# First attention of a two-layer transformer kernel: other work set behind each score round instead of behind each pair of rounds, and the value matmuls set in two halves

## The chip, the core and the metric

The kernel runs on one core of a Trainium2 chip. The metric is the device time of one execution in microseconds (us). Three runs of the kernel before gave a median of 1532.57 us (1531.0 to 1534.91). The engines are named as the profile names them: PE (matmul), PEld (PE's weight load), DVE (vector), ACT (scalar, activations), POOL (GpSimd) and SP (it issues most of the DMAs).

## The reference

The input is x with 64 batch items of 128 tokens and 128 features, a side input `fside` of the same shape and a context `ctx_1024` of 64 x 120 x 128. Four blocks follow each other, each with a layer norm ahead and a residual sum behind. All is float32.

```
def _L0_xattn_ref(x1, x2, memory_k, memory_v, Wq, bq, Wk, bk, Wv, bv, Wp, bp):
    ...
    q = (x1 @ Wq + bq).reshape(Bn, Nq, H, D).transpose(0, 2, 1, 3)
    k = x2 @ Wk + bk
    v = x2 @ Wv + bv
    k = jnp.concatenate([k, memory_k], axis=1)
    v = jnp.concatenate([v, memory_v], axis=1)
    ...
    attn = jnp.einsum('bhqd,bhkd->bhqk', q, k) * scale
    attn = jax.nn.softmax(attn, axis=-1)
    out = jnp.einsum('bhqk,bhkd->bhqd', attn, v)
    ...
    return out @ Wp + bp
...
    x = x + _L0_xattn_ref(_layernorm(x, axis=-1), fside_BxSxS_0, ctx_1024, ctx_1024, ...)
    x = x + _L0_ffn_ref(_layernorm(x, axis=-1), L0_ffn_wqkv, L0_ffn_w1, L0_ffn_w2)
    x = x + _L1_xattn_ref(_layernorm(x, axis=-1), ctx_1024, ctx_1024, ...)
    x = x + _L1_ffn_ref(_layernorm(x, axis=-1), L1_ffn_Wg, L1_ffn_bg, L1_ffn_W1, L1_ffn_W2)
```

Both attentions have 16 heads of 8 features. The first one attends over 248 keys: 128 projected from `fside` and 120 taken from the context as they are. The second attends over 120 keys projected from the context. Both feed-forward blocks send each token to 2 of 8 experts. The change touches the first attention only.

## The kernel before

The kernel runs four stages after each other: loads, the first attention with the first router beside it, the first layer's experts ("tile stage"), and the second attention with the second layer's experts beside it. The order of PE, ACT, DVE and POOL is the order in which the program is written; SP's order is chosen by the framework's scheduler, except at the beginning and at the end of the first attention.

**The pipeline.** `attention` runs a loop over `it` from 0 to 68 (`B + 5` steps for 64 batch items). In each step several batch items are worked on at different depths: item `it` gets its row maxima, item `it-1` its shift, item `it-2` its scores and exponentials, item `it-3` its values and the first two output steps, item `it-4` its third and item `it-5` its last two. Batch items are grouped by four (`GB`), and the projections of the next group are spread over the four steps of a group.

**A round** (`round_`, calling `max_bank` L386 and `score_bank` L418) fills four PSUM banks by eight matmuls that use the PE array in four strips of 32 rows, so that four of them run side by side:

- two "left" banks: query x key for 248 keys (L394), of which DVE takes the negated maximum (`tensor_reduce`, L414) into `nm`,
- two "right" banks: key x query for one chunk of keys, 128 or 120 of them (L430), of which ACT takes the exponential into `p` (L438).

All first matmuls of the four banks are issued ahead of the second ones. A step has four rounds, 0 to 3, so 16 banks. PSUM has eight; every other PE result of the loop takes a bank of the same pool (`mtile`), too, and a bank becomes free when DVE or ACT has read it. Rounds 0 and 1 read the first key chunk, rounds 2 and 3 the second.

**The other work of a step**, with the lines that the prediction uses:

- `shift` (L459 on PE, L462 on DVE): transposes the maxima of item `it-1` and adds them to its queries by two `scalar_tensor_tensor`.
- `values` (L475): exponentials x values, in the array cut into four strips of 32 columns. `values(b, 0)` takes a bank and fills its first half, `values(b, 1)` its second half, 32 matmuls each. `out1` (L484) is ACT's copy of that bank.
- `out2` (L491 on PE, then L495 and L497 on DVE), `out3` (L504 on PE, L506 on ACT), `out4` (L511 on PE), `out5` (L516 on DVE, then the norm statistics L109).
- `aside.ahead` (one more L109 on DVE) and `aside.call`, twice a step: the next pieces of the router. Of PE they hold L176 (with ACT's copy L177) and L681 in one step of four, and L831 in one of eight; the rest is small DVE and POOL work, and POOL's scatters.
- `prep(it, 0)` and `prep(it, 1)`: the next group's projections. By `j = it % 4`: query projection (L292, with ACT's L301 twice in each of the two calls, and its bank held from the first call to the end of the second) at j=0, nothing at j=1, values (L214, DVE's L221) and keys (L202, ACT's L207) at j=2, turned inputs (L176, ACT's L177) at j=3.
- `context`: at j=2, the DMAs of the next group's context keys (L261) and values (L266). `aside.end` issues stores of zeros (L1278) from SP.

A step of the first attention runs: rounds 0 and 1; `out4`, `shift`, `out5`, `ahead`, a router call; both halves of the values and `out1`; `context`, `prep(it, 0)`, a router call; rounds 2 and 3; `out3`, `out2`, `prep(it, 1)`, `aside.end`.

Of the kernel before, what the change touches and what calls it, by code (L numbers as in the profile page):

```python
# [44 lines left out]
def transformer_kernel(ctx, tc, a, out):  # L45
# [186 lines left out]
    def attention(layer, w, norm, first, aside):  # L232
# [5 lines left out]
        with ExitStack() as es:  # L238
# [14 lines left out]
            def loads(g):  # L253
                n = KF if first else KC
                t = work.tile([D, GB, n], F32, name="kvT", tag="kvT")
                nc.sync.dma_start(t, a["fsideT" if first else "ctxT"][:, g * GB : (g + 1) * GB, :])
                src[g] = t
# [13 lines left out]
            def context(g):  # L271
                if first:
                    context_k(g)
                    context_v(g)
# [167 lines left out]
            def round_(ba, bc, rnd):  # L442


                one, two = ((0, 2), (1, 3)) if rnd % 2 == 0 else ((1, 3), (0, 2))
                left = [max_bank(ba, ra, rnd // 2) for ra in one] if ba is not None else []
                right = [score_bank(bc, ra, rnd // 2) for ra in two] if bc is not None else []
                banks = [x for pair in zip(left, right) for x in pair] if left and right else left + right
                for u in range(2):
                    for parts, _ in banks:  # L450
                        parts[u]()
                for _, after_ in banks:
                    after_()
# [12 lines left out]
            def values(b, v):  # L466
                g, j = divmod(b, GB)
                if v == 0:
                    pavs[b] = mtile()
                pav = pavs[b]  # L470
                p = ps_[b]
                for i in range(2):
                    for c, (_, n) in enumerate(chunks):
                        for ra in range(4):
                            nc.tensor.matmul(  # L475
                                pav[32 * ra : 32 * ra + 32, v * S : (v + 1) * S],
                                lhsT=vs[g % 2][c][:, j, 4 * v + ra, i, :],
                                rhs=p[:n, c, ra, (2 * v + i) * S : (2 * v + i + 1) * S],
                                start=(i == 0 and c == 0), stop=(i == 1 and c == nc_ - 1),
                            )  # L480
# [38 lines left out]
            def norm_of(g):  # L519
                if g < NG:  # L520
                    normed[g] = norm.normed(g)
                    biased(g)
# [30 lines left out]
            for it in range(B + 5):  # L553
                def on(back, *steps):
                    b = it - back
                    if 0 <= b < B:
                        for f in steps:
                            f(b)

                def rounds(*which):  # L560
                    ba = it if it < B else None
                    bc = it - 2 if 0 <= it - 2 < B else None
                    for r in which:
                        if ba is not None or bc is not None:
                            round_(ba, bc, r)

                if first and it % GB == 2:
                    norm_of(it // GB + 2)
                if 2 <= it <= B + 1 and it - 2 not in ps_:
                    ps_[it - 2] = work.tile([128, nc_, 4, 512], F32, name="p", tag="p")  # L570
                if it % GB == 0 and 0 < it // GB + 1 < NG:
                    if it:
                        loads(it // GB + 1)
                vals = (lambda b: values(b, 0), lambda b: values(b, 1), out1)
                if first:
                    rounds(0, 1)


                    on(5, out4)
                    on(1, shift)  # L580
                    on(5, out5)
                    aside.ahead(it)
                    aside.call(it, mtile)
                    on(3, *vals)
                    if it % GB == 2 and it // GB + 1 < NG:
                        context(it // GB + 1)
                    prep(it, 0)
                    aside.call(it, mtile)
                    rounds(2, 3)
                    on(4, out3)  # L590
                    on(3, out2)
                    prep(it, 1)
                    aside.end(it, work, mtile)
                else:
                    on(3, *vals)
                    rounds(0, 1)


                    aside.piece(mtile)
                    prep(it, 0)  # L600
                    on(4, out3)
                    on(3, out2)
                    on(5, out4)
                    aside.call(it, mtile)
                    prep(it, 1)
                    on(1, shift)
                    on(5, out5)
                    aside.ahead(it)
                    if it > GB and it % GB == 1:
                        norm_of(it // GB + 1)  # L610
                    aside.fetch_for(it)
                    aside.call(it, mtile)
                ps_.pop(it - 3, None)
                yield
# [676 lines left out]
    wr0 = const.tile([D, 3 * E], F32, name="c_wqkvT", tag="c_wqkvT")  # L1291
    aside0 = Aside0()
    steps = attention(0, l0, norms[0], True, aside0)
    next(steps)
    l0.update(attention_weights("a0_", ("wq", "bq")))
# [170 lines left out]
    with ExitStack() as es:  # L1466
        aside1 = Aside1(es.enter_context(tc.tile_pool(name="yb", bufs=1)))
        with tc.manual_schedule(engines=ORDERED):
            for _ in attention(1, l1, norms[2], False, aside1):
                pass  # L1470
# [91 lines left out]
```

## Time and profile before

| what | value |
|---|---|
| median of three runs | 1532.57 us |
| the profiled execution's own time | 1582.29 us |
| its span, first to last instruction | 1580.5 us |
| mean granted PE clock | 0.973 |
| busy share of the span: PE, PEld | 91%, 71% |
| busy share: DVE, ACT, POOL | 70%, 54%, 41% |
| L414 reduces of both attentions | 768, 465.4 us busy |
| L438 exponentials of both attentions | 768, 403.5 us busy |
| L430, L394 score matmuls, busy | 444.5 us, 294.3 us |
| L475 value matmuls on PE (p,v and p,vc), busy | 179.6 us, 104.2 us |

The span is one profiled execution; the runs that give the median were not profiled and are shorter. A busy PE is not PE at its peak, since matmuls overlap each other. The first attention's loop takes the span from about 30 us to about 630 us. There its steps repeat with a period of eight (two groups), which makes it possible to read one period and to multiply.

### The profile page before, as it was taken

The numbers are of one execution on the slowest core, as the hardware profiler recorded it, in microseconds if no ns is written. First come the engines' busy times: TensorE is split into PE (matmuls) and PEld (weight loads), VectorE is DVE, ScalarE is ACT, GpSimd is POOL, SyncE is SP. The second block draws the span as 40 slices with busy tenths as digits, with TensorE's granted clock in tenths as the row PEclk, the third lists the DMA queues.
The fourth block names the chain that finished last, engine by engine and source line by source line (L and its number), as shares of the span: only waits on it lengthen the run. The fifth ranks groups of instructions, "written<-read, shape, count | busy, mean of one in ns | idle before, by whom it ended". The sixth has DMA issues, their size and how long they took to land.

```text
span 1580.5 us, 41996 instructions
## 1 busy us (share of the span) xinstructions
PE 1442.8 (91%) x16620; PEld 1118.6 (71%) x16620; DVE 1106.3 (70%) x3024; ACT 849.7 (54%) x1740; POOL 641.3 (41%) x1195
## 2 busy tenths in 40 slices
PE   7969999999999999787999999888989898988987
PEld 5757777777777677676888888566666676666765
DVE  6757888888888988354654444688776777777763
ACT  4646666666666666442333333566656565655653
POOL 4122345646465534464001122376555555444210
PEclk9989999999999999899999999899999999999999
DMA  7851222222222221365776676111000111100000
GB/s 192 222 138 46 55 61 68 67 61 64 57 64 58 56 70 37 93 187 173 213 201 189 194 202 180 46 35 30 28 28 28 37 31 31 31 28 15 15 8 28
DMA packets 143719, 133.03 MB, mean 84 GB/s; under 512 B 48546, under 2 KB 126114, under 8 KB 141602
## 3 DMA queue, kind: packets, MB, share of 16 engines
q1 hardware_dynamic: 135330, 113.02, 25.9%
q0 software_dynamic: 8192, 17.32, 3.5%
q8 instruction: 132, 2.16, 0.6%
q14 instruction: 65, 0.53, 0.1%
HBM read 97.32 MB, written 32.97 MB: 82 GB/s over the span
## 4 chain that ended last, share of the span: by engine, by line
PE 66%; DVE 15%; DMA 6%; SPq 5%; issue 3%; ACT 3%; POOL 3%; another core or an unknown queue 0%; POOLq 0%; ACTq 0%; DVEq 0%
PE bank L430 10%; PE bank L475 9%; PE bank L1115 8%; PE bank L394 8%; PE bank L1420 4%; PE bank L1441 4%; DVE nm L414 3%; PE bank L1128 3%; DMA q<-xs 3%; SPq L1278 2%; PE bank L407 2%; PE bank L292 2%; DVE q L462 2%; PE bank L511 2%; PE bank L681 2%
## 5 line engine op out<-in xcount | busy, mean ns | idle before, releaser
L414 DVE TENSOR_REDUCE nm<-bank 128x2 f32<-128x496 f32 (+1 forms) x768 | 465.4, 662 | 100.6 <-PE bank L430 68.6
L438 ACT ACTIVATE p<-bank 120x512 f32<-120x512 f32 (+1 forms) x768 | 403.5, 603 | 154.9 <-PE bank L430 138.5
L430 PE MATMUL bank<-q,k 32*120 32x256 f32 (+1 forms) x3072 | 444.5, 401 | 14.8 <-DVE nm L414 5.0
L430 PEld LDWEIGHTS bank<-q,k 32*120 32x120 f32 (+1 forms) x3072 | 298.3, 182 | 61.9 <-DVE nm L414 16.6
L394 PE MATMUL bank<-k,q 32*128 32x248 f32 x2048 | 294.3, 403 | 12.5 <-DMA k<-in_ctx_k 11.8
L394 PEld LDWEIGHTS bank<-k,q 32*128 32x128 f32 x2048 | 203.1, 190 | 59.7 <-issue 23.0
L475 PE MATMUL bank<-p,v 128*32 128x128 f32 (+1 forms) x4096 | 179.6, 279 | 1.8 <-DVE h L1435 0.6
L1120 DVE TENSOR_TENSOR p<-p,bank 128x256 f32<-128x256 f32 x213 | 87.9, 420 | 125.4 <-ACT p L1119 112.6
L407 PE MATMUL bank<-k,qf 32*128 32x480 f32 x512 | 150.8, 604 | 1.3 <-ACT qf L295 0.8
L807 POOL DMA_INDIRECT xs<-xn,at x128 | 129.2, 1009 | 28.6 <-issue 25.0
L1119 ACT ACTIVATE p<-bank 128x256 f32<-128x256 f32 x213 | 80.9, 384 | 100.9 <-PE bank L1115 91.9
L484 ACT COPY ov<-bank 128x256 f32<-128x256 f32 x128 | 48.0, 375 | 157.5 <-PE bank L475 146.0
L475 PEld LDWEIGHTS bank<-p,v 128*32 128x32 f32 (+1 forms) x4096 | 111.2, 110 | 26.1 <-issue 13.2
L1115 PE MATMUL bank<-q 128*128 128x256 f32 x516 | 122.3, 388 | 4.6 <-ACT q L1106 4.6
L1360 POOL DMA_INDIRECT yb<-ys,back x112 | 108.7, 970 | 27.7 <-issue 19.3
L462 DVE SCALAR_TENSOR_TENSOR q<-bank,c_smask,q 128x256 f32<-128x256 f32 x256 | 111.1, 475 | 10.3 <-PE bank L459 9.6
L167 POOL TENSOR_SCALAR xn<-x,mv,rstd 128x128 f32<-128x128 f32 x252 | 110.6, 452 | 7.3 <-issue 1.3
L1115 PEld LDWEIGHTS bank<-q 128*128 128x128 f32 x516 | 97.4, 196 | 17.3 <-ACT q L1106 5.0
L155 POOL TENSOR_SCALAR rstd<-mv 128x4 f32<-128x4 f32 x32 | 6.4, 199 | 246.7 <-DVE mv L113 150.0
L475 PE MATMUL bank<-p,vc 120*32 120x128 f32 x2048 | 104.2, 272 | 0.6 <-issue 0.5
L1157 POOL DMA_INDIRECT kvT<-ys,back x16 | 15.4, 962 | 197.5 <-DMA vc<-xs 118.1
L301 ACT ACTIVATE q<-bank,c_a_bq,c_hmask 128x512 f32<-128x512 f32 x124 | 90.1, 788 | 9.8 <-PE bank L292 9.8
(224 smaller groups left out, 2477.6 us busy)
## 6 DMA issues: line engine op xcount, KB each, us to landing
q<-in_w SPq DMA_DIRECT2D x43, 576.0 KB
vc<-in_w SPq DMA_DIRECT2D x28, 576.0 KB
vc<-in_ctx_v SPq DMA_DIRECT2D x16, 960.0 KB
ys<-zero SPq DMA_DIRECT2D x71, 128.0 KB
k<-in_ctx_k SPq DMA_DIRECT2D x32, 240.0 KB
q<-xs SPq DMA_DIRECT2D x43, 128.0 KB
ys<-q SPq DMA_DIRECT2D x43, 128.0 KB
x<-in_x SPq DMA_DIRECT2D x16, 256.0 KB
```

The source lines that it names most:

```text
L167: nc.gpsimd.tensor_scalar(xn[:, j, :D], xg[g][:, j, :], self.mv[:, b, 0:1], self.rstd[:, b : b + 1], ALU.add, ALU.mult,)
L301: nc.scalar.activation(q4s[g][:, :, s, :], pq.rearrange("p (b q) -> p b q", b=GB), AF.Identity, bias=w["bq"][:, s : s + 1], scale=hmask[:, ...
L394: nc.tensor.matmul(pa[:, u, :], lhsT=q4s[g][r, j, s, :], rhs=k2[g % 2][r, s // 2, j, :], start=True, stop=True,)
L407: lambda: nc.tensor.matmul(pa, lhsT=qfs[g][r, j, :], rhs=k4s[g][r, :, j, :], start=True, stop=True),
L414: nc.vector.tensor_reduce(nm[b % 2].rearrange("q i (a s) -> q a i s", s=16)[:, 2 * ra + v : 2 * ra + v + len(slots) // 2, :, 0], pa.rearra ...
L430: nc.tensor.matmul(pb[:n, v * 256 : (v + 1) * 256], lhsT=k2[g % 2][r, v, j, k0 : k0 + n], rhs=q4s[g][r, j, 2 * v : 2 * v + 2, :].rearrange ...
L438: nc.scalar.activation(ps_[b][:n, c, ra, :], pb[:n], AF.Exp, scale=SCALE)
L462: nc.vector.scalar_tensor_tensor(q, pm, smask[:, v : v + 1], q, ALU.mult, ALU.add)
L475: nc.tensor.matmul(pav[32 * ra : 32 * ra + 32, v * S : (v + 1) * S], lhsT=vs[g % 2][c][:, j, 4 * v + ra, i, :], rhs=p[:n, c, ra, (2 * v + ...
L807: s = nc.gpsimd.indirect_dma_start(xs, bass.IndirectOffsetOnAxis(at[:, j, k : k + 1], 0), xn, None)
L1115: nc.tensor.matmul(ph[:, u, :], lhsT=w[:, c, u * 128 : (u + 1) * 128], rhs=xT, start=True, stop=True)
L1360: nc.gpsimd.indirect_dma_start(y[:, k, b % 2, :], None, ys, bass.IndirectOffsetOnAxis(back[:, b, k : k + 1], 0),)
```

## The change

Only the order of calls within a step of the first attention changes. Each round of four banks now stands alone, with a part of the other work behind it. The two halves of the values are separated by round 2, the second router call moves ahead of round 2, and `context` and `prep(it, 0)` stay behind the values, now between rounds 2 and 3. Nothing is computed that was not computed before.

```diff
                 if first:
-                    rounds(0, 1)
-
-
+
+                    rounds(0)
                     on(5, out4)
                     on(1, shift)
                     on(5, out5)
                     aside.ahead(it)
                     aside.call(it, mtile)
-                    on(3, *vals)
+                    rounds(1)
+                    on(3, vals[0])
+                    aside.call(it, mtile)
+                    rounds(2)
+                    on(3, *vals[1:])
                     if it % GB == 2 and it // GB + 1 < NG:
                         context(it // GB + 1)
                     prep(it, 0)
-                    aside.call(it, mtile)
-                    rounds(2, 3)
+                    rounds(3)
                     on(4, out3)
                     on(3, out2)
                     prep(it, 1)
```

`vals` is the triple of the first half of the values, the second half, and `out1`.

## Prediction, made before the changed kernel was run

> **What bounds the kernel now.** I read the page first: PE is busy for 91% of the span, DVE for 70%. Then I read the windows of two whole groups (four steps each) in the even part of the first attention, from one first value matmul to the next but three:
>
> ```profile
> 211.50:248.69 37.19, 36.76 (x570) 27.89 (x569) 31.82 (x80) 24.53 (x50) 20.41 (x42) 1.00 0.24 61
> 248.69:287.80 39.11, 37.77 (x574) 28.55 (x573) 32.94 (x86) 24.19 (x50) 20.57 (x49) 1.00 0.23 60
> ```
>
> The columns are window and length, then busy us of PE, PEld, DVE, ACT and POOL, granted clock, DMA share and GB/s. PE looks full (36.8 of 37.2), DVE has 31.8, ACT 24.5. But PE's busy time hides waiting, since matmuls overlap. So next I looked at the timeline of PE for a block of two rounds that nothing holds up:
>
> ```profile
> 242.55 0.47 PE L394 MATMUL bank<-k,q 32*128 32x248 f32 x1
> ...
> 242.86 0.37 PE L394 MATMUL bank<-k,q 32*128 32x248 f32 x1
> ...
> 243.07 0.37 PE L394 MATMUL bank<-k,q 32*128 32x248 f32 x1
> ...
> 244.14 0.37 PE L394 MATMUL bank<-k,q 32*128 32x248 f32 x1
> ...
> 244.45 0.33 PE L504 MATMUL bank<-ident,o 128*128 128x128 f32 x1
> ```
>
> Four matmuls start together; the first four take 0.31 us to the next four, then each 0.21, and the last 0.30 to the next operation. From 242.55 to 244.45 is **1.90 us for two rounds**. Most blocks take longer. The chain of waits says why:
>
> ```profile
> 289.76 1.05 PE bank L292 x2
> 290.82 0.40 PE bank L394
> ...
> 291.90 0.67 DVE nm L414
> 292.57 0.04 issue
> 292.62 0.47 PE bank L430
> 293.11 0.63 PE bank L430 x4
> 293.73 0.26 PE bank L504
> ```
>
> The last bank of rounds 2 and 3 had to wait until DVE had reduced a bank of this same block. From 292.62 the block still needs 1.1 us, as long as a round alone: PE issues in order, so one late bank delays the whole round. The block took 2.91. Rounds 0 and 1 wait for something else, DVE's queue:
>
> ```profile
> 302.21 2.42 DVE L414 TENSOR_REDUCE nm<-bank 128x2 f32<-128x496 f32 x4 [0.77 <-PE bank L430]
> 304.54 0.25 DVE L495 RECIPROCAL rs<-bank 128x16 f32<-128x16 f32 x1
> 304.83 0.29 DVE L497 TENSOR_TENSOR o<-bank,rs 128x128 f32<-128x128 f32 x1
> ```
>
> `out2`'s bank was filled by 303.5 and is free only at 305.1, because four reduces of 0.605 stand ahead of its two DVE steps.
>
> From the same timeline, the 16 blocks of the two groups take (first start to the next operation's start) 2.92, 2.95, 1.91, 2.77, 2.09, 2.66, 1.90, 2.41 and 2.92, 2.96, 1.91, 2.77, 3.37, 2.67, 1.91, 2.61. Over 1.90 each, that is **4.4 us of waiting in the first group and 5.9 in the second**, on average 5.2 of 38.15.
>
> **The change, part by part.**
>
> *Splitting the rounds.* One round alone is 0.31 + 0.21 + 0.21 + 0.30 = 1.03 us; two are 2.06 instead of 1.90. There are two such splits in a step: +0.32. *Splitting the values*: 64 matmuls take 1.90 (298.24 to 300.14 in the chain), at 0.11 for four 1.76, so 0.14 are the way in and out, and two halves pay it twice, about +0.13. Together **+0.45 us in a step, 1.8 in a group**. All of it lies on PE, the engine that sets the pace. The switch from strips of rows to strips of columns is not in the trace; its nearest rows are row strips to whole array (0.30 instead of 0.21) and whole array to column strips (L459 to L475, 0.20 instead of 0.11), so 0.09 to 0.18 above the pace. I take the lower one, as what leaves is the same; the upper adds 0.2 in a step.
>
> Here a rule speaks against the change. The Trainium skill, "TensorEngine Tiling (Array Packing)", section "Tiling Modes", says that changing the tiling mode drains TensorE. A plain step has 5 changes of mode before and 8 after. Taken at its word, nothing of the new mode begins until the last matmul has ended (0.37 after its start instead of 0.21) and the first weights are loaded (0.18): 0.34 a change, 1.0 a step, 4.1 a group. The trace shows less of it: from the last row-strip matmul to L504 are 0.30, weights included. I go by the row.
>
> *The waits.* I laid four steps out by hand from these durations: reduce 0.605 and exponential 0.53 in a row, the first 0.10 and 0.15 after a round's end (301.07 to 302.21 and 302.25 for a round of 1.03); shift's two DVE steps 0.78, `out5` 0.28, two statistics 0.49, reciprocal and product 0.54; 0.4 of router work on DVE for each call (the windows' 64.8 us of DVE for eight steps, less 58 for the named groups, over 16 calls); `out4` and `shift` 0.64 on PE, `out3` and `out2` 0.54; ACT's query steps 0.79 each. Each new bank takes the one longest free.
>
> - Plain step: round 3 ends at 0, round 0 would start at 0.54 and finds two banks free; its last two take round 3's first exponential and first reduce, free at 0.75: wait 0.1 to 0.2. `out4` and `shift` follow, then round 1, which takes the banks of `out3`, `out2` and two of round 0's, free 0.75 after it, when PE is there after 0.64: wait 0.1. Round 2 comes 2 us later and takes round 0's others, `shift`'s and `out4`'s: DVE frees these about 1.9 us after round 0 (two reduces, two shift steps, `out5`), no wait. Round 3 has the second half of the values ahead of it; DVE is through round 1's reduces 0.8 us earlier: no wait, and `out1` comes in time.
> - j=0: the query projection's bank is held over round 3 and to the end of its four ACT steps, and ACT does two of these ahead of round 3's exponentials and two behind. Of the following step round 0 waits 0.8 for the second reduce of round 3, and round 1 waits 0.7 for its fourth bank, since round 0's exponentials start 1.1 late.
> - j=2 into j=3: ACT's two key steps (L207, 0.78 each) hold up round 0's exponentials; round 1 waits 0.6.
>
> Sum over a group: 0.13+0.13 (j=0), 0.83+0.7 (j=1), 0.23+0.13 (j=2), 0.57 (j=3) = **2.7 us**, where 4.4 and 5.9 stood. The first group comes out at 37.19 - 4.4 + 2.7 + 1.8 = 37.3, the second at 39.11 - 5.9 + 2.7 + 1.8 = 37.7: **0.65 us less a group on average**. The bounds: no waiting at all (5.2 - 1.8 = 3.4 less) and waiting undiminished (1.8 more).
>
> *Moved work.* The second router call goes ahead of round 2: its DVE work now stands ahead of round 2's reduces, which have about 0.8 us to spare; L681 then gives DVE and ACT a microsecond there. `context` now waits for round 2 as well, about 1 us later in its step; its keys are read in round 0 two steps (18 us) on, its values later still, so nothing waits. The weight of ACT's idle time ahead of `out1` (83 us waiting for L475 in all) goes, worth nothing, as ACT isn't late there. The shift of item `it-1` now has one round less ahead of it: it needs round 3's reduces, done at 1.3 to 1.5 after round 3, and comes at 1.9; half a microsecond is left.
>
> *Where it counts.* Up to 95.6 us the loop doesn't run free. SP's queue:
>
> ```profile
> 52.67 39.79 SPq L1278 DMA_DIRECT2D ys<-zero  x63
> 92.56 1.04 SPq L261 DMA_DIRECT2D k<-in_ctx_k  x2
> ```
>
> The keys for step 8 are issued behind 63 stores of zeros; PE stands from 83.9 to 95.6. A faster or slower step ahead of it changes only that wait. So steps 8 to 63 count, 14 groups: 14 x 0.65 = **9 us less**. The profiled execution goes from 1582.3 (span 1580.5, 1.8 around it) to 1573. The 50 us by which it exceeds the median I can't place; as the attention runs at clock 1.00 in the profile, I carry the 9 us over: 1532.6 - 9 = 1524.
>
> **The rivals.**
>
> - *The waits all but vanish* and PE's own work with the splits is the bound: 14 x 3.4 = 48 less, 1485. For it: DVE (32.4 a group) and ACT are below PE. Against: at j=0 and j=2 ACT's extra steps stand in its queue whatever the order.
> - *The drain costs what the rule says* (slower): three more changes of mode a step at 0.34. The layout removes 0.62 us of waiting a step (5.2 - 2.7 over four), so the change loses once its switches cost more than that; at 1.0 it is 0.4 x 56 = 22 more, 1555. For it: the direct switch between row and column strips, twice a step, is in no row. Against: all rows of other switches.
> - *SP's order changes*: the scheduler may put the keys of step 8 ahead of the zeros, 11.7 us less on top, 1512, or more zeros ahead of some other load. Little speaks for it, as the zeros have no one to wait for in either order.
>
> **How the numbers follow.** Forecast (1524, its own range 1511 to 1536, as each wait of the layout may be off by 0.1 to 0.2 us): 0.54. No waits: 0.09. Drain: 0.32. SP's order: 0.05. What a measurement here can tell from no change is about 0.3%, 4.6 us. Of the forecast's share 0.33 is faster by more than that, 0.16 within and 0.05 slower; with 0.09 and 0.04 faster by the others, that makes 0.46 faster, 0.17 within and 0.37 slower (the drain's 0.32 in it). The range runs from 1500, halfway to the case without waits, to 1558, a little past the drain's.
>
> **What would show it.** In the profile after, a round alone takes 1.03 where it doesn't wait; the switch from L430 to L475 shows 0.30 (right) or 0.5 and more (drain). Waits of a round for DVE's L497 go; the long ones left stand at j=0 to j=1 and end with L414 or L301. The two groups become nearly equal in length. It is wrong if DVE is late for round 3 in plain steps, or if `shift` waits for `nm`.

## The result, and the profile after

The changed kernel is slower: 1551.14 us median of 4 runs (1549.27 to 1554.21) against 1532.88 for the kernel before beside it, ratio **1.0121 [1.0099, 1.0143]**. The forecast was 1524.

Its profiled execution took 1549.27 us with a span of 1547.4. One fact has to stand ahead of every comparison. The same unchanged kernel takes 1533 to 1536 us on some chips and 1581 to 1590 on others. By its time, the profile of before that the prediction works with (1582) belongs to the second kind; the median to be forecast, and the profile after, belong to the first. Profiling is not what makes the difference: the profiled execution of after is the fastest of its four. I call the two kinds **short-time** and **long-time** chips and compare only within a kind. A later run gave a profile of before on a short-time chip (own time 1533.83, span 1532.1), and it is what I set beside the profile after. Each engine's busy time, first of after, then of before on the short-time chip:

```profile
PE 1450.3 (94%) x16620; PEld 1100.3 (71%) x16620; DVE 1100.5 (71%) x3024; ACT 853.3 (55%) x1740; POOL 639.9 (41%) x1195
```

```profile
PE 1425.8 (93%) x16620; PEld 1110.9 (73%) x16620; DVE 1102.1 (72%) x3024; ACT 847.5 (55%) x1740; POOL 640.5 (42%) x1195
```

PE is 24.5 us busier, and the others do about as much as before. The windows of two whole groups show the same, in the same order (window and length, then busy us of PE, PEld, DVE, ACT and POOL, granted clock, DMA share, GB/s):

```profile
257.10:295.95 38.85, 38.30 (x576) 27.36 (x572) 32.77 (x89) 24.30 (x49) 20.81 (x50) 1.00 0.23 61
295.95:334.50 38.55, 38.30 (x572) 27.29 (x568) 31.17 (x76) 24.77 (x49) 22.40 (x47) 1.00 0.24 62
```

```profile
250.30:288.00 37.70, 37.19 (x576) 28.34 (x572) 32.82 (x86) 24.01 (x49) 20.54 (x49) 1.00 0.24 63
288.00:325.20 37.20, 36.77 (x572) 27.82 (x568) 31.55 (x80) 24.32 (x49) 22.73 (x46) 1.00 0.24 64
```

A pair of groups takes 77.4 us where it took 74.9. The last score matmul of the first attention (L430) starts at 649.5 us in after and at 631.7 in before, 17.8 later; behind it both need 898 to 900 us. So the whole loss lies in the first attention.

Where a group's time goes on PE, each block taken from its first start to the next operation's start, mean of the same seven groups in both (us):

| | before | after | difference |
|---|---|---|---|
| score matmuls, unhindered (8 x 1.905; 16 x 1.07) | 15.24 | 17.12 | +1.88 |
| score matmuls, waiting | 4.34 | 3.82 | -0.52 |
| value matmuls (L475) | 7.70 | 8.14 | +0.44 |
| all else | 10.20 | 9.67 | -0.53 |
| group | 37.48 | 38.75 | +1.27 |

The split costs 2.3 us a group, and the waits that should have paid for it went down by only 0.5. 14 such groups would make 14 x 1.27 = 17.8 us, but that this is just the measured 17.8 is chance. From the query projection (L292) at 101.3 us in before and 103.5 in after to the one at 554.9 and 568.1 lie twelve groups, and they lose 11.0 us: the last two of them lose nothing (37.7 and 42.2 us in before, 37.6 and 40.9 in after). 2.2 us are lost ahead of them and 4.6 behind.

A round alone can be read in PE's timeline of after (start, duration, engine, line, operation, count):

```profile
267.91 0.47 PE L394 MATMUL bank<-k,q 32*128 32x248 f32 x1
...
268.22 0.37 PE L394 MATMUL bank<-k,q 32*128 32x248 f32 x1
...
268.43 0.37 PE L394 MATMUL bank<-k,q 32*128 32x248 f32 x1
...
268.64 0.38 PE L394 MATMUL bank<-k,q 32*128 32x248 f32 x2
...
268.98 0.33 PE L504 MATMUL bank<-ident,o 128*128 128x128 f32 x1
```

The steps are 0.31, 0.21, 0.21 and 0.34, in all 1.07 us. The last one was forecast at 0.30, and it is as long where L475 follows.

The longest new wait is in the chain of waits of after (start, duration, engine, what), in a step with j=0:

```profile
289.62 1.24 DVE nm L414 x2
290.86 0.78 DVE q L462 x2
291.64 0.21 DVE x L516
...
291.87 0.49 DVE st L109 x2
292.36 0.15 DVE flat L843
...
292.54 0.31 DVE sums L844
...
292.87 0.18 DVE start L850
...
293.07 0.17 DVE filled L852
293.25 0.60 DVE nm L414
...
293.89 0.47 PE bank L430
```

Round 2 started at 292.64 and stood from its fourth bank on until 293.89: 1.22 us more than its 1.07. The kernel's pool has eight banks (L240, `bufs=8`), and this one had been used by round 1, which PE had finished at 291.62. DVE came to reduce it only at 293.25, since between round 0's last reduces and this one its queue held `shift` (L462), `out5` (L516), two statistics (L109) and a router call (L843 to L852). In program order all of that now stands *ahead* of round 1, and round 1's reduces come behind it.

The other things foretold can be read in the same views. The stores of zeros stay ahead of the keys in SP's queue, so no head start is won (SP's timeline of after):

```profile
51.82 39.85 SPq L1280 DMA_DIRECT2D ys<-zero  x63
91.78 1.05 SPq L261 DMA_DIRECT2D k<-in_ctx_k  x2
```

### The profile page after: what moved, and what is told of

It reads as the page before. It is cut to its first block, busy times and chain, and to the rows that moved or that the text cites. A ratio compares the mean times of both kernels' runs of the same rounds, so it can differ in the third digit from the quotient of the medians.

```text
span 1547.4 us, 42001 instructions
## 1 busy us (share of the span) xinstructions
PE 1450.3 (94%) x16620; PEld 1100.3 (71%) x16620; DVE 1100.5 (71%) x3024; ACT 853.3 (55%) x1740; POOL 639.9 (41%) x1195
## 4 chain that ended last, share of the span: by engine, by line
PE 65%; DVE 16%; DMA 6%; SPq 4%; POOL 4%; ACT 3%; issue 2%; POOLq 0%; DVEq 0%; ACTq 0%
PE bank L394 12%; PE bank L1117 9%; PE bank L475 8%; PE bank L430 7%; DVE nm L414 4%; PE bank L1422 4%; PE bank L1443 4%; PE bank L1130 3%; SPq L1280 2%; DVE q L462 2%; DMA q<-xs 2%; PE bank L407 2%; PE bank L683 2%; DMA vc<-xs 2%; PE bank L214 2%
## 5 line engine op out<-in xcount | busy, mean ns | idle before, releaser
L414 DVE TENSOR_REDUCE nm<-bank 128x2 f32<-128x496 f32 (+1 forms) x768 | 470.4, 662 | 115.0 <-PE bank L430 88.8
L438 ACT ACTIVATE p<-bank 120x512 f32<-120x512 f32 (+1 forms) x768 | 412.2, 601 | 244.1 <-PE bank L430 210.8
L430 PE MATMUL bank<-q,k 32*120 32x256 f32 (+1 forms) x3072 | 472.5, 404 | 9.9 <-DVE nm L414 5.0
L430 PEld LDWEIGHTS bank<-q,k 32*120 32x120 f32 (+1 forms) x3072 | 296.3, 182 | 46.3 <-DVE q L462 15.4
L394 PE MATMUL bank<-k,q 32*128 32x248 f32 x2048 | 316.1, 411 | 9.0 <-DMA k<-in_ctx_k 7.5
L394 PEld LDWEIGHTS bank<-k,q 32*128 32x128 f32 x2048 | 195.0, 192 | 73.3 <-issue 30.1
L475 PE MATMUL bank<-p,v 128*32 128x128 f32 (+1 forms) x4096 | 178.1, 279 | 0.7 <-ACT p L438 0.5
L475 PEld LDWEIGHTS bank<-p,v 128*32 128x32 f32 (+1 forms) x4096 | 104.4, 110 | 55.5 <-issue 45.4
L1117 PE MATMUL bank<-q 128*128 128x256 f32 x516 | 118.6, 380 | 0.7 <-ACT q L1108 0.7
L462 DVE SCALAR_TENSOR_TENSOR q<-bank,c_smask,q 128x256 f32<-128x256 f32 x256 | 111.1, 475 | 8.4 <-PE bank L459 7.7
L475 PE MATMUL bank<-p,vc 120*32 120x128 f32 x2048 | 103.3, 272 | 0.0
L138 POOL TENSOR_TENSOR mv<-st 128x4 f32<-128x4 f32 x31 | 6.4, 205 | 209.7 <-DVE st L109 209.7
```

The lines of the kernel that those rows point to most:

```text
L394: nc.tensor.matmul(pa[:, u, :], lhsT=q4s[g][r, j, s, :], rhs=k2[g % 2][r, s // 2, j, :], start=True, stop=True,)
L414: nc.vector.tensor_reduce(nm[b % 2].rearrange("q i (a s) -> q a i s", s=16)[:, 2 * ra + v : 2 * ra + v + len(slots) // 2, :, 0], pa.rearra ...
L430: nc.tensor.matmul(pb[:n, v * 256 : (v + 1) * 256], lhsT=k2[g % 2][r, v, j, k0 : k0 + n], rhs=q4s[g][r, j, 2 * v : 2 * v + 2, :].rearrange ...
L438: nc.scalar.activation(ps_[b][:n, c, ra, :], pb[:n], AF.Exp, scale=SCALE)
L462: nc.vector.scalar_tensor_tensor(q, pm, smask[:, v : v + 1], q, ALU.mult, ALU.add)
L475: nc.tensor.matmul(pav[32 * ra : 32 * ra + 32, v * S : (v + 1) * S], lhsT=vs[g % 2][c][:, j, 4 * v + ra, i, :], rhs=p[:n, c, ra, (2 * v + ...
```

## The experiments

Two theories were set against each other. The **queue theory**: round 2 waits since round 1's reduces stand behind `shift`, `out5`, the statistics and a router call on DVE; an order that puts all of this but `shift` behind round 1 brings the time back. The **price theory**, the prediction's second rival: the split itself (more changes of PE's mode) costs the time, whatever the order. Each ratio is against before on the same chip.

**Round 1 ahead of the DVE work; each half of the change alone** (a long-time chip, before 1581.82). In the first, against after:

```diff
                     on(1, shift)
+                    rounds(1)
                     on(5, out5)
                     aside.ahead(it)
                     aside.call(it, mtile)
-                    rounds(1)
                     on(3, vals[0])
```

In the second, only rounds 0 and 1 are split (against before):

```diff
-                    rounds(0, 1)
+                    rounds(0)
...
                     aside.call(it, mtile)
+                    rounds(1)
                     on(3, *vals)
```

In the third, only the values, rounds 2 and 3 and the second call are as in after:

```diff
-                    on(3, *vals)
+                    on(3, vals[0])
+                    aside.call(it, mtile)
+                    rounds(2)
+                    on(3, *vals[1:])
...
                     prep(it, 0)
-                    aside.call(it, mtile)
-                    rounds(2, 3)
+                    rounds(3)
```

And the kernel before unchanged, for its spread:

> The unchanged kernel once more. Its profile tells whether the 33 us by which the profile of the changed kernel is shorter than that of before come from code that the change doesn't touch: expected is a span of 1530 to 1535 us with the stages behind the first attention as long as in the changed kernel's profile (334 and 556 us), and the two groups of the first attention again 37.2 and 39.1 us. If the span is 1580 again, the profile of before was no exception. Time: no change, 1533.

> The changed kernel, with out5, ahead and the first router call moved behind round 1, so that round 1's reduces follow the shift directly in DVE's queue. Theory Q (round 2 waits for round 1's first reduce, which stands behind out5, the statistics and the router call): the waits of round 2 (about 1.7 us a group, 1.2 of it at j=0) mostly go, some 16 groups give 15 to 20 us, 1533. Theory D (the price is that of the split rounds and values themselves): the waits are made up elsewhere and the time stays within 5 us of 1551.

> Only rounds 0 and 1 are parted (out4, shift, out5, ahead and the router call between them); the values stay whole and rounds 2 and 3 together. Theory D: one split pair costs 0.23 us a step more than before (1.07 twice for 1.91), 15 us over 64 steps, 1548. Theory Q: round 1 comes 0.65 us later, so that out2's bank is mostly free for it (0.4 us less waiting a step) and the values, 1.9 us long, cover round 1's late reduces: 0.15 a step less in all, about 1523.

> Only rounds 2 and 3 and the values are parted, rounds 0 and 1 stay together as before. Theory D: 0.23 + 0.14 us a step more, 24 us, 1557. Theory Q: round 1's reduces stand ahead of the shift and of out5 in DVE's queue, so round 2 doesn't wait, and out2's two DVE steps have two reduces ahead of them, not four (0.5 us less waiting a step for rounds 0 and 1): 0.15 a step less in all, about 1523.

Measured: unchanged 0.9995 [0.9976, 1.0013]; DVE work late 1.0101 [1.0074, 1.0127]; first half alone 1.0011 [0.9992, 1.0029]; second half alone 1.0049 [1.0029, 1.0068].

The halves alone cost little: not the 1.0 and 1.6% that the price theory gave them, and without the 0.6% less that the queue theory gave them. After as a whole costs 1.7% on a long-time chip (below), so it is the combination that costs. With the DVE work late, every second group fell to 37.8 us, without a wait of round 2, but the groups between rose to 41.2. Such a rise is in the second half alone too. PE's timeline of that kernel, and a line of DVE's:

```profile
280.42 0.40 PE L475 MATMUL bank<-p,vc 120*32 120x128 f32 x8
281.81 0.41 PE L831 MATMUL bank<-m,c_upper 128*128 128x64 f32 x2 [0.99 <-DVE s L748]
```

```profile
281.46 0.21 DVE L820 TENSOR_TENSOR m<-one,one 128x64 f32<-128x64 f32 x1
```

The router's product L831 is the next thing in PE's queue and needs DVE's `m`, which DVE reaches at 281.46, after `shift`, `out5` and the statistics (the row names L748, DVE's next instruction). With the second call right behind the first half of the values, two router calls follow each other closely, and the second one's matmul comes before DVE is ready. In the kernel with the DVE work late this wait is 1.1 us of such a group, and `out2` (L491) waits 1.0 for ACT's copy. So the queue theory had to be tested with the calls kept apart.

**The calls kept apart** (a short-time chip, before 1535.46). To "DVE work late" and to the second half alone, the same edit:

```diff
                     on(3, vals[0])
-                    aside.call(it, mtile)
                     rounds(2)
...
                     prep(it, 0)
+                    aside.call(it, mtile)
                     rounds(3)
```

In the first half alone, the second call goes from behind `prep(it, 0)` to right behind the values. And the changed kernel once more.

> The changed kernel once more, on the same chip as the next three, whose times are to be set against it. The profile of before so far came from a chip on which before takes 1582 us, that of after from one on which before takes 1533. Both theories expect a ratio of 1.012 and a first attention that ends 10 us later than that of before (last L430 at 649 instead of 639 us). If PE's standing without a releaser in the value matmuls, seen in the parts of the change, belongs to the chip, it shows here too; in the first profile of after there was none.

> The changed kernel with out5, ahead and the first router call behind round 1, and the second router call behind prep(it, 0) as before the change. In the run before with the router calls close to each other, L832 waited 1.1 us for the m that the first call makes on DVE, and ACT 1.1 us longer, in every second group; with two microseconds more between the calls both should go. Theory Q: the waits of round 2 stay away in both kinds of group, which come out at 37.8 and 38.0 us (after: 38.6 and 38.9), 1.000 of before. Theory D (the splits' own price decides, waits only move): 1.010.

> Rounds 2 and 3 and the values parted, rounds 0 and 1 together, and the second router call left behind prep(it, 0). With the call ahead of round 2, this part cost 1.005, and in every second group L831 waited 1.06 us for DVE's m and out2 1.09 for ov. If the moved call is what costs there, both go, and the ratio is 0.997 to 0.999. If the split itself costs, it stays at 1.004 to 1.006.

> Rounds 0 and 1 parted as in the run before, and the second router call ahead of prep(it, 0), behind the whole values. The call is two microseconds of PE behind the first one here, so that its move should cost nothing: the groups stay at 37.2 and, if PE stands again for 1.8 us in the values of every second group, 39.3. If that standing goes by the place of the instructions in PE's stream, it moves or goes: then 37.5 for the second kind and a ratio of 0.992 to 0.996; otherwise 1.001.

Measured: after again 1.0112 [1.0095, 1.0129]; DVE work late, calls apart **1.0011 [1.0002, 1.0019]**; second half, calls apart 0.9996 [0.9984, 1.0008]; first half, call early 0.9976 [0.9965, 0.9987].

This decides between the theories. The kernel with 1.0011 has every split of the changed kernel, and the same lone rounds and half values; only the order, DVE's work behind round 1 and the calls apart, differs. Its groups are 37.8 and 37.2 us, its waits of score rounds 2.46 us a group where after has 3.82, and none of them is in round 2. In DVE's timeline of that kernel, in the same kind of step as the chain above:

```profile
286.81 1.26 DVE L414 TENSOR_REDUCE nm<-bank 128x2 f32<-128x496 f32 x2 [0.32 <-PE bank L430]
287.99 0.86 DVE L462 SCALAR_TENSOR_TENSOR q<-bank,c_smask,q 128x256 f32<-128x256 f32 x2
288.89 1.26 DVE L414 TENSOR_REDUCE nm<-bank 128x2 f32<-128x496 f32 x2
290.06 0.28 DVE L516 TENSOR_TENSOR x<-x,bank 128x128 f32<-128x128 f32 x1
```

and in PE's:

```profile
289.85 0.47 PE L394 MATMUL bank<-k,q 32*128 32x248 f32 x1
...
290.92 0.43 PE L475 MATMUL bank<-p,v 128*32 128x128 f32 x8
```

Round 1's reduces begin at 288.89, directly behind `shift`, and `out5` and the statistics come behind them. Round 2 starts at 289.85 and takes 1.07: no wait.

**Is it the place of the call alone?** (a long-time chip, before 1590.48, and another, before 1588.69.) The second call moved in before alone; round 1 pulled ahead of `out5` with rounds 2 and 3 kept together; the second call put back behind `prep(it, 0)` in after; the best version once more.

```diff
                     on(3, *vals)
+                    aside.call(it, mtile)
...
                     prep(it, 0)
-                    aside.call(it, mtile)
                     rounds(2, 3)
```

is the edit of the first, against before. The second has `rounds(0)`, `out4`, `shift`, `rounds(1)`, `out5`, `ahead`, the first call, the values, the second call, and the rest as before.

> The unchanged kernel. The second set of runs was on a chip where before takes 1535 us and no profile of before from such a chip exists. If its groups are 37.2 and 39.1 us as in both profiles so far, theory Q can't explain the measured 1.011: the attention would give 9 us and 8 us would have to come from the stages behind. If the second kind of group is 37.7 here, as in all parts of the change that ran on that chip, before has 37.5 on average, the changed kernel's 38.75 cost 14 x 1.25 = 17.5 us, and all of the measured 16 to 18 us lies in the first attention. Time: no change.

> Before with only the second router call moved ahead of context and prep(it, 0). No theory gives it a cost where the whole values stand between the calls: 0.998 to 1.001. If the gain of the run with rounds 0 and 1 parted and the call moved came from the call's move, it shows here as 0.9975.

> Rounds 0 and 1 parted, the values whole, the second router call behind them, and out5, ahead and the first router call behind round 1. Theory Q: in this form round 1's reduces weren't late for anything, since the whole values and prep lie ahead of round 2, so nothing is gained by moving DVE's work: 0.996 to 0.999, groups 37.0. If DVE's order matters beyond round 2's waits (round 0 of the next step), the groups fall under 36.8.

> The unchanged kernel, once more in search of its profile on a chip where it takes some 1535 us; both calls with its profile met chips where it takes 1580 to 1590. On a fast chip: the first kind of group 37.2, the second 37.7 instead of 39.2 (the forecast was made from a profile in which the second kind holds 1.4 us of waiting that belongs to the chip). On a slow chip: 37.2 and 39.2 again. Time: no change.

> The changed kernel with only the second router call put back behind prep(it, 0). The run that cured round 2's waits made two edits at once, DVE's order and this one. Theory Q: the call has no part in the waits of round 2 at j=0 and j=3, where round 1's reduces stand behind out5, the statistics and the first call; the ratio stays at 1.009 to 1.012. If the moved call is the cause, it falls to 1.001.

> Rounds 0 and 1 parted, the values whole, the second router call behind them. It was at 0.9976 on a fast chip; on a slow one its sister with the call behind prep(it, 0) was at 1.001, with 1.8 us of standing in the values of every second group. On a fast chip again 0.997 to 0.998. On a slow chip 0.997 as well if the standing is the same for before and for this, 1.000 to 1.002 if it hits this order harder.

Measured: unchanged 1.0001 [0.9989, 1.0014] and 1.0000 [0.9987, 1.0014]; call alone 0.9991 [0.9979, 1.0003]; round 1 early, rounds 2 and 3 together 1.001 [0.9999, 1.0022]; after with the call put back **1.0206 [1.0185, 1.0228]**; first half with early call 1.0036 [1.0024, 1.0048].

The place of the second call is not the cure: put back in the changed kernel it takes nothing from the loss (after itself has 1.0169 on the long-time chip of the next runs).

The kernel that cured the waits holds two edits, and neither was run alone on a short-time chip. Their traces separate them all the same. In the second of the twelve groups counted above, which ends between 175 and 180 us, before takes 37.2 us on both kinds of chips, and so the long-time chip doesn't disturb it. That group takes 38.4 in after and 38.4 with the call put back, of which round 2 waits 1.7 in both; it takes 37.2 with the DVE work late and 37.2 with both edits, and round 2 waits in neither. This is its last round 2, first with the call put back, then with the DVE work late:

```profile
175.77 0.47 PE L394 MATMUL bank<-k,q 32*128 32x248 f32 x1
...
176.72 0.47 PE L430 MATMUL bank<-q,k 32*120 32x256 f32 x1 [0.25 <-DVE nm L414]
...
177.77 0.42 PE L475 MATMUL bank<-p,v 128*32 128x128 f32 x8
```

```profile
174.38 0.47 PE L394 MATMUL bank<-k,q 32*128 32x248 f32 x1
...
175.44 0.42 PE L475 MATMUL bank<-p,v 128*32 128x128 f32 x8
```

So the order on DVE alone takes the waits of round 2 away. Keeping the calls apart matters in the groups with L831: the next group takes 38.9 with the DVE work late, with 1.1 of waiting ahead of L831, and 37.8 with both edits.

The version that was 0.24% faster than before is 0.36% slower on a long-time chip, so none was found that beats both kernels on both kinds of chips.

**The cure on a long-time chip** (before 1580.98).

> The unchanged kernel. On a chip where it takes 1535 us: second kind of group 37.7 us. On one where it takes 1580 to 1590: 39.2 us again, as in four profiles.

> The changed kernel. On a fast chip 1.011 again. On a slow one the question is what its waits do there: with the second router call put back it took 1.021 on such a chip, groups of 40.3 and 41.9 us. Theory Q: the call's place is not the cause, so 1.015 to 1.022 and groups over 40.

> The changed kernel with DVE's work behind round 1 and the second router call behind prep(it, 0). On a fast chip 1.001 again. On a slow one theory Q expects that it still takes away most of what the change costs: 1.000 to 1.006, the first kind of group 37.2 to 37.5.

Measured: unchanged 1.0003 [0.9987, 1.0019]; after 1.0169 [1.0145, 1.0193]; DVE work late, calls apart 1.0048 [1.0033, 1.0063]. On one chip, the two edits together take away 1.2 of the 1.7%; on a short-time chip they took away 1.0 of 1.1%. (On long-time chips the DVE work late alone had 1.0101, the call alone 1.0206.) What is left on the long-time chip isn't explained in full: from about 215 us on, its groups are 37.8 to 38.2 and 38.3, against 37.8 and 37.2 on the short-time one, so that it is mainly the shorter kind that grows.

**The kernel before on a short-time chip**, one profiled run.

> The kernel before once more, for its profile. If the chip is one on which it takes about 1533 to 1535 us, theory (the profile on record came from another chip, whose odd groups hold 1.4 us more): groups of 37.2 and 37.7 us, their difference one wait for the router's product, 75 us a pair less than 1 us apart. Rival (before's groups are 37.2 and 39.2 on every chip): 37.2 and 39.2. On a chip on which it takes about 1580 to 1590 us both expect 37.2 and 39.2, and the question stays open.

It took 1533.83 us beside 1535.86 of the kernel before on the same chip (one run each). Its groups are 37.70 and 37.20, shown above. The five profiles of before from long-time chips have 37.2 and, but for one of 38.4, 39.1 to 39.3, though only from 250 us on; ahead of that they have the groups of the short-time chip. So the excess of the longer group, which the prediction took for something the change would remove, belongs to the long-time chips, and even in the prediction's own profile the pair that it read doesn't stand for the whole loop.

## Why the prediction failed, step by step

**The base was wrong.** "As the attention runs at clock 1.00 in the profile, I carry the 9 us over" is a step that doesn't hold. The clock was 1.00, but the two groups averaged 38.15 us on that chip and 37.45 on a chip of the kind where the median was taken. In the blocks this is mainly one block at j=2: 3.37 us on the long-time chip, 2.03 on the short-time one. The waits to be won there were 4.3 in *both* kinds of group, not 4.4 and 5.9. In the prediction's sum that is 14 x 0.7 = 10 us of the miss of 27 (from 9 less to 18 more); in the two profiles of before, the last L430 lies 7.7 us apart (639.4 and 631.7). The forecast's own group of 37.5 us would then have meant no change.

**"Round 2 comes 2 us later and takes round 0's others, `shift`'s and `out4`'s ... no wait" is the step that failed.** Its fourth bank in steps with j=0 is one that round 1 had used. The layout gave the DVE work its due times from round 0 and did not ask where round 1's own reduces stand in DVE's queue. Round 2 waits 1.63 us in the one kind of group (0.41 at j=3, 1.22 at j=0) and 1.91 in the other (0.17 at j=1, 0.49 at j=2, 0.33 at j=3, 0.92 at j=0); forecast were none. The chain above shows the cause for the longest of these; the shorter ones go with the same edit. With the DVE work behind round 1 and the calls apart all of them are gone, the waits are 2.46 a group (forecast 2.7), the group 37.53 (forecast 37.5), and the time is before's within 0.11%. So the layout fits an order which the change doesn't have. The prediction's own signs of being wrong named DVE late for round 3 and `shift` waiting for `nm`; neither came, and round 2 was not among them.

**The cost of splitting was mis-sized.** A lone round takes 1.07 and not 1.03, as leaving row strips takes 0.34 and not 0.30. The prediction's own lines hinted at it: with steps of 0.31, six times 0.21 and 0.30 two rounds come to 1.87, and they took 1.90, partly because the 0.30 was counted from the last of the four matmuls that start together. 16 lone rounds make +1.88 a group against 1.28 forecast, 8 us over 14 groups. The values gave +0.44 against 0.52. Together it is 0.58 in a step where I had 0.45. Row strips to column strips, in no row of before, turned out no dearer than row strips to whole array.

**The other waits.** Round 0 at j=1 was forecast at 0.8 and measured at 0.89; round 1 at j=1 at 0.7 and measured at none; round 1 at j=3 at 0.6, measured 0.35. Round 0 at j=0, forecast as a plain step with 0.1, took 0.45. Not forecast at all were 0.5 us a group saved in the operations between the blocks, mostly behind L491.

**The moved work.** The prediction feared the second call for its DVE work ahead of round 2's reduces. In the changed kernel that did no harm, as putting it back shows; its early place cost where no more than half the values lay between the two calls (L831: DVE work late, second half alone). What hurt is the *first* call, with `out5` and the statistics, which the diff leaves where they were: round 1 was moved past them. How much each of the three does was not told apart. The order on SP stayed, as forecast.

**The drain rival** named 1555, which is near the measured time by luck, as the cause is another. From the rule in the Trainium skill ("TensorEngine Tiling (Array Packing)", section "Tiling Modes") that a change of mode drains TensorE, I had estimated 1.0 us a step; the splits were measured at 0.58. And the kernel that makes all the same changes of mode ends at 1.0011. The price is real, and it takes what the waits give back; it doesn't make the loss. The rival without waits is refuted: 2.46 us a group stay in the best order of all these splits.

## What to carry to other kernels

When work is split and interleaved on one engine, write out the order on *every* in-order engine again: a step that the diff doesn't touch (here DVE's `out5`, statistics and first call) may now stand ahead of the work that frees the next buffer. Ask of each buffer a round needs who used it last and what stands ahead of that user's reader in its queue. And before subtracting from a profile, see that its time agrees with the median to be forecast; 50 us that can't be placed may be the very time one hopes to win.

## What the runs showed of the hardware that was not expected

**Chips differ for the same code.** Before took 1533 to 1536 us on short-time chips (4 and 14 in the record) and 1581 to 1590 on long-time ones (2, 13 and 15). Only chip 13 was met twice, with 1588.69 and 1580.98, so that the difference belongs to the chip itself is likely, but not shown. In the first attention only every second group is longer, from 250 us on (37.7 and 39.2); in the second attention the longer groups take 34.4 us on the one kind and 38 to 39 on the other. The granted clock doesn't explain it: in the groups of the first attention it is 1.00 on both, and in the second a group of 38.7 us on the long-time chip has 0.98 where one of 34.4 on the short-time chip has 1.00.

**PE stands inside a dense run of value matmuls, in runs on long-time chips alone.** The first half of the change alone shows it in PE's timeline:

```profile
267.34 0.97 PE L475 MATMUL bank<-p,v 128*32 128x128 f32 x7
268.63 0.29 PE L475 MATMUL bank<-p,v 128*32 128x128 f32 x1 [0.32 <-issue]
268.64 0.42 PE L475 MATMUL bank<-p,vc 120*32 120x128 f32 x4
269.37 0.43 PE L475 MATMUL bank<-p,vc 120*32 120x128 f32 x4 [0.31 <-issue]
```

The 64 matmuls took 3.75 us instead of 1.90, with nothing that the profile shows to wait for ("issue"). The same place comes back in each second group from 249 us on, and with it the gain of the early call is lost there: on the short-time chip these values take 1.90. In before on a long-time chip it is DVE that stands near this place: it begins L221 at 272.26, 1.38 us after the end of PE's last L214, whose bank it reads; on the short-time chip it begins 0.04 after it. The instruction queue's packets, of 16 KB, fall near such places (one from 267.60 to 268.84 here), but in after on the short-time chip they fall near L475 as well (one from 266.76 to 267.89) and nothing stands. Whether fetching instructions is the cause stays open, as does what sets the two kinds of chips apart; no run here could separate it.
